# GroupNorm attention block on one core: score bursts of three units, one PSUM bank for all projection chains, x reloaded by blocks, VectorE in written order

## The chip, the cores and the metric

One NeuronCore of a Trainium2 chip runs the whole program. The metric is the device time of one execution in microseconds (us). TensorE (PE) does the matrix products, VectorE (DVE) the elementwise work, ScalarE (ACT) the exponentials, GpSimd (POOL) some small elementwise work and some DMA issues, SyncE (SP) most DMA issues. Each engine takes its instructions in order and waits on semaphores of the others.

## The reference

Four images of 512 channels and 48 x 48 = 2304 positions; eight heads of 64 channels.

```python
hn = _group_norm(x, gn_scale, gn_bias)                    # 32 groups of 16 channels
qkv = jnp.einsum('oc,bchw->bohw', qkv_w, hn) + qkv_b[None, :, None, None]
q, k, v = ...                                             # float16, (b, head, 64, 2304)
w = jnp.einsum('bhct,bhcs->bhts', q * scale, k * scale)
w = jax.nn.softmax(w, axis=-1)
a = jnp.einsum('bhts,bhcs->bhct', w, v).astype(jnp.float32)
out = jnp.einsum('oc,bchw->bohw', proj_w, a) + proj_b[None, :, None, None]
return x + out
```

## The kernel before, in words

`kernel` launches one program, in which `fast_path` does everything; `general_path` runs only if a softmax sum falls out of range, which does not happen here. The work is cut by image `b` (4), pair of heads `g` (16 in all, 4 an image) and block `j` of queries (`QBLOCKS`: four of 512 positions and one of 256).

**Attention.** A unit is one tile of 128 keys for both heads of a pair and 512 queries (for the block of 256 queries: two key tiles). `scores` makes the two matmuls of a unit (`ps`, a tile of two PSUM banks; the two heads use 64 rows of the array each), ACT's exp turns them into `p` (float16, 128x1024), and DVE adds `p` to `acc`. `values` multiplies `p` by `v` and accumulates in `av`, one PSUM bank for the whole block (here the two heads use 64 columns of the array each). A block of 512 queries has 18 units, the block of 256 has 9. Units come in bursts of two: PE gets the scores of burst n, then the values of burst n-1. After each six units `add_up` multiplies `acc` by ones into `sl` (a bank of its own) and `finish` copies the sums out, takes them through DRAM to spread them over partitions (`sums`, `row`, `ib`, all on SP's queue) and lets POOL scale the block (`att`).

**Work beside it.** Between bursts `fill` issues pieces from the list `beside[b]`, as many as keep a share of the list proportional to the place in the image: q and k chains of later pairs (`qk_items`: four steps over the channels into one bank `pw`, then a DVE eviction), v chains of the next image (`v_items`), projection chains of the image before (`proj_items`, eight float32r matmuls, a DVE add of bias and residual, a store). `pw` has two banks, `ps` two tiles (four banks), `av` and `sl` one bank each: eight in all.

**The turn between images.** `load_x` reloads x whole: four tiles of 2304 columns, each with one buffer, so its DMAs, issued from POOL, wait for the last q/k chain that reads the tile. `turn` puts the load and `norm_stats` after the chains of pair 3, `norm_apply` comes later in the list: `gmean` and `gvar` are matmuls in PE's order, and the v chains behind them need the normalised x.

**Order.** PE runs in the order in which the code issues (a manual schedule). All other engines' order is chosen by the scheduler.

Of the kernel before, what the change touches and what calls it, by code (L numbers as in the profile page):

```python
# [30 lines left out]
SCALE = float(np.float16(1.0 / math.sqrt(math.sqrt(D))))  # L31
LAG = 2
SUMMED = 6
# [10 lines left out]
SB = 384  # L44
# [422 lines left out]
def fast_path(  # L467
# [18 lines left out]
    apool = ctx.enter_context(tc.tile_pool(name="apool", bufs=7))  # L486
    ppool = ctx.enter_context(tc.tile_pool(name="ppool", bufs=6))
# [9 lines left out]
    def load_x(b, engines):  # L497
        chunks = []
        for c in range(NC):
            t = xpool.tile([P, T], F32, tag=f"x{c}", name=f"x_{b}_{c}")  # L500
            for h in range(2):
                cols = bass.ts(h, T // 2)
                engines[h].dma_start(t[:, cols], x[b, bass.ts(c, P), cols])
            chunks.append(t)
        return chunks

    hn = {0: load_x(0, (nc.sync, nc.scalar))}
# [28 lines left out]
    def split_wproj():  # L536
        for c in range(NC):
            w = work.tile([P, C], F32, tag="res", bufs=3, name=f"wproj_{c}")
            nc.sync.dma_start(w, proj_wT[bass.ts(c, P), :])
            nc.vector.tensor_copy(whi[:, c, :], w)  # L540
            nc.vector.tensor_tensor(
                wlo[:, c, :], w, whi[:, c, :].bitcast(F32), ALU.subtract
            )
# [22 lines left out]
    bqk = const.tile([P, 2 * NC], F32, name="bqk")  # L566
    nc.vector.tensor_scalar(bqk, bqkv[:, : 2 * NC], SCALE, None, ALU.mult)

    sums = const.tile([P, NG, 2 * NT], F32, name="sums")


    mvs = {}

    def norm_stats(b):
        mv = small.tile([P, NC, 2], F32, tag="mv", name=f"mv_{b}")
        for c in range(NC):
            st = small.tile([P, T // SB, 6], F32, tag="st", name=f"st_{b}_{c}")
            for j in range(T // SB):
                nc.vector.bn_stats(st[:, j, :], hn[b][c][:, bass.ts(j, SB)])  # L579
            nc.vector.bn_aggr(mv[:, c, :], st.rearrange("p j s -> p (j s)"))  # L580
        mvs[b] = mv

    def norm_apply(b):
        mv = mvs.pop(b)
        pm = ps_w.tile([P, NC], F32, tag="pw", name=f"gmean_{b}")
# [9 lines left out]
        pv = ps_w.tile([P, NC], F32, tag="pw", name=f"gvar_{b}")  # L595
# [11 lines left out]
        for o, n in QBLOCKS:  # L607
            for c in range(NC):
                t = hn[b][c][:, o : o + n]
                nc.vector.tensor_scalar(  # L610
                    t, t, ga[:, c : c + 1], gb[:, c : c + 1], ALU.mult, ALU.add
                )
# [4 lines left out]
    def qk_items(g):  # L617
        b, pr = divmod(g, NPAIR)
        items = []

        def new():
            qk[g] = [
                qkp.tile([P, T], F16, tag=n, name=f"{n}_{g}") for n in ("q", "k")
            ]

        def one(part, j, c, pw):
            o, n = QBLOCKS[j]
            if c == 0:
                pw[0] = ps_w.tile([P, QB], F32, tag="pw", name=f"pqk_{g}_{part}_{j}")
            w0 = part * C + pr * P  # L630
            for lo in (0, D):
                nc.tensor.matmul(  # L632
                    pw[0][lo : lo + D, :n],
                    wqkv[:, c, w0 + lo : w0 + lo + D],
                    hn[b][c][:, o : o + n],
                    start=(c == 0),
                    stop=(c == NC - 1),
                )
            if c == NC - 1:
# [3 lines left out]
                    pw[0][:, :n],  # L643
                    SCALE,
                    bqk[:, col : col + 1],
                    ALU.mult,
                    ALU.add,
                )

        items.append((0.0, new))  # L650
        for part in (1, 0):
            for j in range(NQ):
                pw = {}
                for c in range(NC):
                    items.append(
                        (
                            QBLOCKS[j][1] / 600.0,
                            lambda part=part, j=j, c=c, pw=pw: one(part, j, c, pw),
                        )
                    )  # L660
        return items
# [4 lines left out]
    def v_items(b):  # L666
        items = []

        def new():
            vv[b] = [  # L670
                vpool.tile([P, NT, C // 2], F16, tag=f"v{i}", bufs=1 + i, name=f"v{i}_{b}")
                for i in range(2)
            ]

        def one(i, c, pw):
            if c == 0:
                pw[0] = ps_w.tile([P, QB], F32, tag="pw", name=f"pv_{b}_{i}")
            for lo in (0, D):
                nc.tensor.matmul(  # L679
                    pw[0][lo : lo + D, :],  # L680
                    hn[b][c][:, i * P + lo : i * P + lo + D],
# [11 lines left out]
        items.append((0.0, new))  # L693
        for i in range(NT):
            pw = {}
            for c in range(NC):
# [109 lines left out]
    def add_up(g, j, m, per, last):  # L806
# [14 lines left out]
        if last:  # L821
            finish(g, j)
# [185 lines left out]
```

## Time and profile before

| | |
|---|---|
| median of 3 runs | 1920.93 us (1920.51 to 1924.32) |
| profiled execution | 1923.01 us, its span 1921.2 us |
| PE busy | 1725.2 us, 90% of the span |
| DVE, ACT, POOL busy | 1169.0, 1250.2, 180.2 us |
| mean granted TensorE clock | 0.978 of full speed |
| first scores start | 128.23 us |

The span runs from the first to the last instruction of the profiled execution. Busy time of PE is modelled from pipelined matmuls, so 90% is not 90% of its peak rate; the time from one group's start to the next group's start tells more than the busy time.

### The profile page before, as it was taken

How to read it: one execution, taken by the hardware profiler on the slowest of the kernel's cores; microseconds unless marked ns; L12 is line 12 of the kernel's file. 1: busy time of each engine (PE TensorE's matmuls, PEld its weight loads, DVE VectorE, ACT ScalarE, POOL GpSimd, SP SyncE). 2: the span in 40 equal slices, each digit the busy share in tenths (PEclk: the TensorE clock that was granted, in tenths of full speed). 3: DMA queues.
4: the chain of work that ended last, by engine and by line, in shares of the span. 5: the costliest groups of instructions: out<-in, count | busy, mean ns of one | idle time of the engine just before them, and what ended most of it. 6: DMA issues, size and time to landing. Idle time of an engine off the chain costs nothing.

```text
span 1921.2 us, 28172 instructions
## 1 busy us (share of the span) xinstructions
PE 1725.2 (90%) x10644; PEld 633.4 (33%) x10644; DVE 1169.0 (61%) x1936; ACT 1250.2 (65%) x1297; POOL 180.2 (9%) x204
## 2 busy tenths in 40 slices
PE   3999998599999998989999999789999998999875
PEld 1332323133333333433233332342323343333333
DVE  5236666666656657676665655767556665567654
ACT  0027777387777775667677767557777877778662
POOL 1000001100000001220000000221000011010111
PEclk9999999799999999999999999999999999999998
DMA  5000001100000003420000000540000021030223
GB/s 203 1 1 12 12 10 57 62 13 15 12 15 12 12 10 131 136 61 13 9 12 15 12 9 12 187 130 7 15 12 12 15 78 31 18 88 13 82 64 102
DMA packets 87730, 82.23 MB, mean 43 GB/s; under 512 B 50720, under 2 KB 56864, under 8 KB 87584
## 3 DMA queue, kind: packets, MB, share of 16 engines
q1 hardware_dynamic: 82848, 62.75, 11.8%
q0 software_dynamic: 3632, 14.18, 2.0%
q10 hardware_dynamic: 1104, 3.41, 0.5%
q8 instruction: 85, 1.39, 0.3%
q14 instruction: 61, 0.50, 0.1%
HBM read 60.83 MB, written 19.17 MB: 42 GB/s over the span
## 4 chain that ended last, share of the span: by engine, by line
PE 68%; ACT 10%; issue 8%; DVE 8%; DMA 5%; POOL 1%; SPq 0%; ACTq 0%; DVEq 0%; POOLq 0%
PE pqk L632 20%; PE ps L757 14%; PE av L792 12%; PE pv L679 10%; ACT p L765 10%; PE pr L720 7%; PE sl L814 3%; DVE acc L778 2%; DVE x L610 1%; DMA x<-x_dram 1%; DVE avx L801 1%; DMA wproj<-proj_wT_dram 1%; DMA sums<-slx 1%; DVE st L579 1%; DMA ib<-row 1%
## 5 line engine op out<-in xcount | busy, mean ns | idle before, releaser
L765 ACT ACTIVATE p<-ps 128x1024 f16<-128x1024 f32 x1296 | 1248.9, 1024 | 633.9 <-PE ps L757 628.0
L778 DVE TENSOR_TENSOR acc<-acc,p 128x1024 f16<-128x1024 f16 x848 | 611.4, 721 | 259.5 <-ACT p L765 242.8
L632 PE MATMUL pqk<-x,wqkv 128*64 128x512 f32 (+1 forms) x2560 | 564.1, 554 | 3.0 <-DVE x L610 2.9
L757 PE MATMUL ps<-q,k 64*128 64x512 f16 (+1 forms) x2880 | 434.7, 363 | 49.4 <-ACT p L765 37.6
L792 PE MATMUL av<-p,v 128*64 128x512 f16 (+1 forms) x2880 | 410.2, 368 | 59.3 <-DVE avx L801 58.8
L757 PEld LDWEIGHTS <-k 64*128 64x128 f16 x2880 | 116.7, 94 | 543.3 <-issue 535.2
L679 PE MATMUL pv<-wqkv,x 128*64 128x512 f32 x1152 | 276.4, 601 | 7.6 <-DVE x L610 7.6
L778 DVE TENSOR_TENSOR acc<-p,p 128x1024 f16<-128x1024 f16 x224 | 160.2, 715 | 179.0 <-ACT p L765 178.5
L844 POOL TENSOR_TENSOR att<-avx,ib 128x512 f16<-128x512 f32 (+1 forms) x80 | 106.5, 1331 | 1506.3 <-DMA ib<-row 1333.0
L632 PEld LDWEIGHTS pqk<-x,wqkv 128*64 128x64 f32 x2560 | 177.7, 138 | 185.1 <-issue 111.8
L792 PEld LDWEIGHTS <-v 128*64 128x64 f16 x2880 | 132.8, 109 | 249.5 <-issue 232.1
L720 PE MATMUL pr<-a,whi 128*128 128x512 f32 (+1 forms) x320 | 127.5, 406 | 11.2 <-POOL a L710 10.8
L720 PE MATMUL pr<-a,wlo 128*128 128x512 f32 (+1 forms) x320 | 119.1, 379 | 0.0
L679 PEld LDWEIGHTS pv<-wqkv,x 128*64 128x64 f32 x1152 | 81.1, 139 | 113.2 <-issue 82.4
L814 PE MATMUL sl<-acc,ones 128*64 128x512 f16 (+1 forms) x512 | 92.1, 377 | 0.1
L727 DVE SCALAR_TENSOR_TENSOR x<-pr,bproj,x 128x512 f32<-128x512 f32 (+1 forms) x80 | 55.6, 695 | 59.6 <-PE pr L720 45.7
L689 DVE TENSOR_TENSOR v<-pv,bv 128x256 f16<-128x256 f32 x144 | 55.9, 417 | 54.9 <-PE pv L679 54.5
L828 DVE COPY slx<-sl 128x512 f32<-128x512 f32 (+1 forms) x80 | 50.9, 637 | 51.6 <-PE sl L814 50.2
L720 PEld LDWEIGHTS pr<-a,whi 128*128 128x128 f32 x320 | 61.8, 193 | 46.6 <-issue 16.7
L641 DVE TENSOR_SCALAR q<-pqk,bqk 128x512 f16<-128x512 f32 (+1 forms) x80 | 55.4, 693 | 27.6 <-PE pqk L632 26.8
L641 DVE TENSOR_SCALAR k<-pqk,bqk 128x512 f16<-128x512 f32 (+1 forms) x80 | 55.2, 690 | 19.3 <-PE pqk L632 18.2
L801 DVE COPY avx<-av 128x512 f32<-128x512 f32 (+1 forms) x80 | 50.8, 635 | 26.0 <-PE av L792 25.7
(46 smaller groups left out, 288.9 us busy)
## 6 DMA issues: line engine op xcount, KB each, us to landing
x<-x_dram SPq DMA_DIRECT2D x64, 256.0 KB, 2.9
ib<-row SPq DMA_DIRECT2D x128, 128.0 KB, 3.0
out_dram<-x SPq DMA_DIRECT2D x64, 256.0 KB, 2.4
x<-x_dram POOLq DMA_DIRECT2D x24, 576.0 KB, 7.1
x<-x_dram ACTq DMA_DIRECT2D x4, 576.0 KB, 11.0
x<-x_dram SPq DMA_DIRECT2D x4, 576.0 KB, 10.7
wqkv<-qkv_wT_dram SPq DMA_DIRECT2D x2, 1024.0 KB, 15.9
sums<-slx SPq DMA_DIRECT2D x128, 2.0 KB, 2.0
```

What stands on the lines that cost most here:

```text
L632: nc.tensor.matmul(pw[0][lo : lo + D, :n], wqkv[:, c, w0 + lo : w0 + lo + D], hn[b][c][:, o : o + n], start=(c == 0), stop=(c == NC - 1),)
L641: nc.vector.tensor_scalar(qk[g][part][:, o : o + n], pw[0][:, :n], SCALE, bqk[:, col : col + 1], ALU.mult, ALU.add,)
L679: nc.tensor.matmul(pw[0][lo : lo + D, :], hn[b][c][:, i * P + lo : i * P + lo + D], wqkv[:, c, 2 * C :], start=(c == 0), stop=(c == NC - 1),)
L689: nc.vector.tensor_tensor(vv[b][half][:, i, :], pw[0][:, cols], bv[:, cols], ALU.add)
L720: nc.tensor.matmul(ps[:, :n], w[:, c, bass.ts(m, P)], at[0][:, c, :n], start=(c == 0 and i == 0), stop=(c == NC - 1 and i == 1),)
L757: nc.tensor.matmul(ps[:, h, a * n : (a + 1) * n], k[rows, bass.ts(i, P)], q[rows, o : o + n], start=True, stop=True,)
L765: nc.scalar.activation(pt, ps, AF.Exp)
L778: nc.vector.tensor_tensor(acc[key], before, pt, ALU.add)
L792: nc.tensor.matmul(av[0][lo : lo + D, :n], vv[b][pr // 2][:, i, pr % 2 * P + lo : pr % 2 * P + lo + D], pt[:, h, a * n : (a + 1) * n], sta ...
L801: nc.vector.tensor_copy(avx[g, j][:, :n], av[0][:, :n])
L814: nc.tensor.matmul(sl[0][lo : lo + D, :n], ones16, t[:, h, a * n : (a + 1) * n], start=(m < SUMMED and a == 0), stop=(last and a == per - 1),)
L844: nc.gpsimd.tensor_tensor(atts[g][:, o : o + n], avx.pop((g, j))[:, :n], ib[:, :n], ALU.mult)
```

## The change

The diff touches almost all of `fast_path`; its core:

```diff
+BURST = 3
-SUMMED = 6
-    apool = ctx.enter_context(tc.tile_pool(name="apool", bufs=7))
-    ppool = ctx.enter_context(tc.tile_pool(name="ppool", bufs=6))
+    apool = ctx.enter_context(tc.tile_pool(name="apool", bufs=6))
+    ppool = ctx.enter_context(tc.tile_pool(name="ppool", bufs=3))
...
-    ps_s = ctx.enter_context(tc.tile_pool(name="ps_s", bufs=2, space=PSUM))
+    ps_s = ctx.enter_context(tc.tile_pool(name="ps_s", bufs=3, space=PSUM))
     ps_av = ctx.enter_context(tc.tile_pool(name="ps_av", bufs=1, space=PSUM))
-    ps_l = ctx.enter_context(tc.tile_pool(name="ps_l", bufs=1, space=PSUM))
-    ps_w = ctx.enter_context(tc.tile_pool(name="ps_w", bufs=2, space=PSUM))
...
+    ps_w = ctx.enter_context(tc.tile_pool(name="ps_w", bufs=1, space=PSUM))
...
+    def load_x(b, j, engines):
...
+        o, n = QBLOCKS[j]
         for c in range(NC):
...
+            t = xpool.tile([P, n], F32, tag=f"x{c}_{j}", name=f"x_{b}_{c}_{j}")
+            engines[c % len(engines)].dma_start(t, x[b, bass.ts(c, P), o : o + n])
+            hn[b, c, j] = t
...
+    alone = [True]
+
+    def chain_bank(name):
+        if alone[0]:
+            return ps_s.tile([P, 2, QB], F32, tag="ps", name=name)[:, 0, :]
+        return ps_w.tile([P, QB], F32, tag="pw", name=name)
...
     def scores(u):
...
+        pt = ppool.tile([P, BURST, 2, QB], F16, tag="p", name=f"p_{g}_{j}_{k}")
+        for r in range(BURST):
+            ps = ps_s.tile([P, 2, QB], F32, tag="ps", name=f"ps_{g}_{j}_{k}_{r}")
...
+            nc.scalar.activation(pt[:, r], ps, AF.Exp)
...
+    def add(u):
...
+        if k == 1:
+            acc[g, j] = work.tile(
+                [P, BURST, 2, QB], F16, tag="acc", bufs=1, name=f"acc_{g}_{j}"
+            )
+        nc.vector.tensor_tensor(acc[g, j], before, pt, ALU.add)
+
+    def add_up(g, j):
+        o, n = QBLOCKS[j]
+        per = QB // n
+        sl = chain_bank(f"sl_{g}_{j}")
...
         for j in range(NQ):
+            for part in (1, 0):
+                put(b, qk_chain(g + 3, part, j), per_pair - 1, g + 3)
+            put(b, [piece(0.0, lambda b=b, j=j: load_x(b + 1, j, (nc.gpsimd,)))])
+            if j > 1:
+                put(b, [piece(0.0, lambda b=b, j=j: stats(b + 1, j - 2))])
...
+    def fill(n, close):
...
+            if after > place or (first and ended):
+                break
+            if done[b] > share and not (close and open_chain[0]):
+                break
...
+        if 0 < n <= len(stream):
+            values(stream[n - 1])
+            add(stream[n - 1])
+        if ended(n - 3):
+            divide(*stream[n - 3][:2])
+        if ended(n - 2):
+            add_up(*stream[n - 2][:2])
+        else:
+            fill(n, ended(n - 1))
...
-    with tc.manual_schedule(engines={mybir.EngineType.PE}):
+    with tc.manual_schedule(engines={mybir.EngineType.PE, mybir.EngineType.DVE}):
```

What it does, in words. Bursts have three units in three `ps` tiles (six banks); `acc` and `p` are 3072 columns wide, so one DVE add takes a burst. `sl` is made once a block, from the 3 x 2 slices of `acc`, and uses the one bank `pw`, which all q, k, v and projection chains share. A `fill` ends at most one chain, and a burst that has an `add_up` has no `fill`. Where the attention is not running (`alone`: the start and the end), chains use the `ps` tiles. x lies in 20 tiles by block, each reloaded as soon as the q and k chains of pair 3 on its block are issued; `stats` follows two blocks later, then `group_mean`, `group_var`, and `norm` block by block among the v chains. Projection chains fetch their residual two chains ahead. The split of the projection weights (`split_wproj`) is spread over the first pair. The range test of the sums is four small POOL instructions a block. DVE, too, runs in the order of the code.

PE, pair 1 of image 0, the boundary between query blocks 1 and 2 (`av_1_1` and `av_1_2`; numbers after the last underscore are buffers; each pair of load and matmul stands twice, once a head). Before:

```order
L757 MATMUL ps_1_2_2_1885<-q_1_632,k_1_633 128x512
L632 MATMUL pqk_3_1_2_1891<-x_0_0_99,wqkv_115 64x512 x2
...
L792 MATMUL av_1_1_1694<-p_1_1_17_1863,v0_0_319 64x512
L792 LDWEIGHTS v0_0_319
L792 MATMUL av_1_2_1898<-p_1_2_0_1869,v0_0_319 64x512
...
L757 MATMUL ps_1_2_3_1901<-q_1_632,k_1_633 128x512
```

The same place in the changed kernel:

```order
L820 MATMUL av_1_1_1646<-p_1_1_5_1768,v0_0_336 64x512
L655 MATMUL pqk_3_0_1_1788<-x_0_3_1_110,wqkv_140 64x512 x2
L796 LDWEIGHTS k_1_552
L796 MATMUL ps_1_2_1_0_1829<-q_1_551,k_1_552 128x512
...
L796 MATMUL ps_1_2_1_1_1833<-q_1_551,k_1_552 128x512
...
L796 MATMUL ps_1_2_1_2_1837<-q_1_551,k_1_552 128x512
...
L820 MATMUL av_1_2_1841<-p_1_2_0_1795,v0_0_336 64x512
```

The first values of the new block stood right behind the last of the old one; now the rest of a chain and the scores of three units stand between them. In PE's order of the kernel before, 40 of the 80 blocks begin inside a burst in this way.

DVE, the turn from image 1 to image 2. Before (`st`: statistics, `acc`: additions, `avx`: copy of `av`):

```order
L778 TENSOR_TENSOR acc_5_3_0_6009<-acc_5_3_0_6009,p_5_3_2_6014 128x1024
L579 BN_STATS st_2_0_6033<-x_2_0_6020 128x6 x3
L727 SCALAR_TENSOR_TENSOR x_0_0_0_6071<-pr_0_0_0_6070,bproj_114,x_0_0_0_6071 128x512
L579 BN_STATS st_2_0_6033<-x_2_0_6020 128x6 x3
L579 BN_STATS st_2_1_6041<-x_2_1_6023 128x6
L580 BN_AGGR mv_2_6032<-st_2_0_6033 128x2
L579 BN_STATS st_2_1_6041<-x_2_1_6023 128x6 x2
L801 COPY avx_5_2_6085<-av_5_2_5821 128x512
L579 BN_STATS st_2_1_6041<-x_2_1_6023 128x6 x3
```

The same turn in the changed kernel (`q_7`, `k_7`: the last chains that read image 1's x; the fourth number of x is its block):

```order
L664 TENSOR_SCALAR q_7_5551<-pqk_7_0_4_5962,bqkv_138 128x256
L589 BN_STATS st_2_5786<-x_2_0_2_5778 128x6
...
L853 TENSOR_TENSOR acc_5_3_5874<-acc_5_3_5874,p_5_3_4_5942 128x3072
L743 SCALAR_TENSOR_TENSOR r_0_3_0_5465<-pr_0_3_0_6011,bproj_139,r_0_3_0_5465 128x512
L829 COPY avx_5_3_6049<-av_5_3_5836 128x512
L853 TENSOR_TENSOR acc_5_3_5874<-acc_5_3_5874,p_5_3_5_5991 128x3072
L743 SCALAR_TENSOR_TENSOR r_0_3_1_5498<-pr_0_3_1_6052,bproj_139,r_0_3_1_5498 128x512
L589 BN_STATS st_2_5786<-x_2_0_3_5900 128x6
...
L872 COPY slx_5_3_6108<-sl_5_3_6101 128x512
L853 TENSOR_TENSOR acc_5_4_6144<-p_5_4_0_6024,p_5_4_1_6069 128x3072
L888 RECIPROCAL inv_5_3_6152<-sums_5_3_6110 128x8
```

The statistics of a whole image stood almost in a row, a burst's work between them; now four of one block stand between the adds and evictions of several bursts, and the reciprocal, which waits for a DMA, has a fixed place behind an add.

## Rows read from the trace of the kernel before

**Rows 1.** The page: busy time, share and count of each engine.
```profile
PE 1725.2 (90%) x10644; PEld 633.4 (33%) x10644; DVE 1169.0 (61%) x1936; ACT 1250.2 (65%) x1297; POOL 180.2 (9%) x204
```
**Rows 2.** Timeline of PE, 700 to 722 us: start us, us, group [idle before <-releaser].
```profile
702.85 0.60 PE L757 MATMUL ps<-q,k 64*128 64x512 f16 x4
703.38 0.62 PE L792 MATMUL av<-p,v 128*64 128x512 f16 x4
703.84 1.88 PE L632 MATMUL pqk<-x,wqkv 128*64 128x512 f32 x8
705.65 0.61 PE L757 MATMUL ps<-q,k 64*128 64x512 f16 x4
...
719.90 0.39 PE L792 MATMUL av<-p,v 128*64 128x512 f16 x2
721.35 0.41 PE L792 MATMUL av<-p,v 128*64 128x512 f16 x2 [1.06 <-DVE avx L801]
```
**Rows 3.** Waits of PE, 128 to 1890 us: total us, times, longest us.
```profile
PE av L792 <- DVE avx L801: 58.8, 41, 7.3
PE ps L757 <- ACT p L765: 37.6, 82, 0.9
PE gmean L586 <- DVE mv L580: 20.1, 1, 20.1
```
**Rows 4.** Windows: length, busy by engine (count), granted clock, DMA share, GB/s.
```profile
330.00:360.00 30.00, 6.42 (x42) 2.80 (x40) 20.00 (x50) 3.46 (x4) 5.44 (x8) 0.56 0.46 167
...
1200.00:1300.00 100.00, 81.36 (x478) 41.71 (x478) 72.46 (x132) 53.07 (x57) 23.62 (x31) 0.93 0.48 152
```
**Rows 5.** Timeline of all engines, first turn, 328 to 352 us.
```profile
328.68 1.28 POOL L503 DMA_DIRECT2D x<-x_dram  x2 [14.33 <-PE pqk L632]
...
342.95 1.63 POOL L503 DMA_DIRECT2D x<-x_dram  x3
347.01 1.48 DVE L579 BATCH_NORM_STATS2 st<-x 128x6 f32<-128x384 f32 x3 [4.96 <-DMA x<-x_dram]
...
351.96 0.59 PE L586 MATMUL gmean<-mv,gmat 128*128 128x4 f32 x2 [20.10 <-DVE mv L580]
```
**Rows 6.** Timeline of all engines, the start and the first scores.
```profile
21.81 0.56 PE L586 MATMUL gmean<-mv,gmat 128*128 128x4 f32 x2 [21.81 <-DVE mv L580]
26.22 0.43 DVE L540 CAST whi<-wproj 128x512 fp32r<-128x512 f32 x1 [4.55 <-DMA wproj<-proj_wT_dram]
...
29.89 0.59 PE L596 MATMUL gvar<-var,gmat 128*128 128x4 f32 x2 [7.51 <-DVE var L594]
...
33.42 33.07 PE L632 MATMUL pqk<-x,wqkv 128*64 128x512 f32 x160 [2.95 <-DVE x L610]
...
128.23 0.61 PE L757 MATMUL ps<-q,k 64*128 64x512 f16 x4
```
**Rows 7.** Timeline of all engines, last image, 1871 to 1890 us.
```profile
1871.03 0.39 PE L720 MATMUL pr<-a,whi 128*128 128x512 f32 x1
...
1872.89 0.40 PE L720 MATMUL pr<-a,whi 128*128 128x512 f32 x1
...
1876.72 0.60 PE L757 MATMUL ps<-q,k 64*128 64x512 f16 x4
...
1877.21 7.44 ACT L765 ACTIVATE p<-ps 128x1024 f16<-128x1024 f32 x8 [8.98 <-PE ps L757]
...
1886.50 1.15 SPq L832 DMA_DIRECT2D sums<-slx  x2
...
1889.21 0.20 DVE L834 RECIPROCAL inv<-sums 128x8 f32<-128x8 f32 x1 [0.40 <-DMA sums<-slx]
...
1889.76 1.07 ACT L765 ACTIVATE p<-ps 128x1024 f16<-128x1024 f32 x1
```
**Rows 8.** Groups by form: count, busy us, mean ns, idle before us, releasers.
```profile
L778 DVE TENSOR_TENSOR acc<-acc,p 128x1024 f16<-128x1024 f16 x848 | 611.4, 721 | 259.5 <-ACT p L765 242.8 <-DVE acc L778 0.5 <-DVE inv L834 0.2
L778 DVE TENSOR_TENSOR acc<-p,p 128x1024 f16<-128x1024 f16 x224 | 160.2, 715 | 179.0 <-ACT p L765 178.5
...
L641 DVE TENSOR_SCALAR q<-pqk,bqk 128x512 f16<-128x512 f32 x64 | 47.8, 746 | 22.7 <-PE pqk L632 21.8
...
L641 DVE TENSOR_SCALAR q<-pqk,bqk 128x256 f16<-128x256 f32 x16 | 7.7, 478 | 5.0 <-PE pqk L632 5.0
```
**Rows 9.** The chain that ended last: start us, us, what.
```profile
66.50 61.80 PE pv L679 x288
```

More of the change, by code (lines that the diff above doesn't have):

```diff
@@ L824, in finish @@
-    def finish(g, j):
+                    sl[lo : lo + D, :n],
+                    ones16,
+                    t[:, r, h, a * n : (a + 1) * n],
+                    start=((r, a) == steps[0]),
+                    stop=((r, a) == steps[-1]),
+                )
+        sx = work.tile([P, QB], F32, tag="rows", name=f"slx_{g}_{j}")
+        nc.vector.tensor_copy(sx[:, :n], sl[:, :n])
+        sums[g, j] = small.tile([P, 2, QB // P], F32, tag="sums", name=f"sums_{g}_{j}")
+        for h in range(2):
+            nc.sync.dma_start(sums[g, j][:, h, : n // P], sx[h * D : h * D + 1, :n])
@@ new lines, in fast_path, with issue @@
+    done = dict.fromkeys(range(B), 0.0)
+    open_chain = [False]
+    def issue(b):
+        us, run, first, last, _, _ = beside[b].pop(0)
+        run()
+        done[b] += us
+        open_chain[0] = (open_chain[0] or first) and not last
+    def fill(n, close):
+        b, place = min(n // per_batch, B - 1), n
+        place = n - b * per_batch
+        share = total[b] * (place + 1) / (per_batch - 2)
+        ended = False
+        while beside[b]:
+            _, _, first, last, after, _ = beside[b][0]
+            if after > place or (first and ended):
+                break
+            if done[b] > share and not (close and open_chain[0]):
+                break
@@ L931, in fast_path @@
-    for u in waiting:
-        values(u)
-    while late:
-        late.pop(0)()
+    ended = lambda n: 0 <= n < len(stream) and stream[n][3]
+    for n in range(len(stream) + 4):
+        if n < len(stream):
+            wanted(stream[n][0])
+            scores(stream[n])
+        else:
+            alone[0] = True
+        if 0 < n <= len(stream):
[5 more added lines that the diff above has]
+            add_up(*stream[n - 2][:2])
+        else:
+            fill(n, ended(n - 1))
@@ L948, in fast_path @@
-    pf = ps_w.tile([1, 1], F32, tag="pw", name="count")
-    for i in range(2):
-        nc.tensor.matmul(
-            pf, good[:, i : i + 1], ones, start=(i == 0), stop=(i == 1)
-        )
-    nc.vector.tensor_scalar(flag, pf, float(B * HEADS * T) - 0.5, None, ALU.is_lt)
+    good = small.tile([P, 1], F32, tag="good", bufs=1, name="good")
+    nc.vector.tensor_reduce(good, fine.rearrange("p h i -> p (h i)"), AX.X, ALU.add)
+    pf = chain_bank("count")[:1, :1]
+    nc.tensor.matmul(pf, good, ones, start=True, stop=True)
@@ L956, in group_norm_attention @@
+    nc.vector.tensor_scalar(flag, pf, float(2 * QB) - 0.5, None, ALU.is_lt)
 @with_exitstack
```

498 lines of the change are left out of this document (253 added, 245 removed).

## The prediction

> **What bounds the kernel now.** I read the page first [rows 1]: PE is busy for 1725 of 1921 us, ACT for 1250 and DVE for 1169. So PE bounds it; but what its busy time is made of, the timeline shows better. I price PE's work by the distance between starts. In the first image's v chains nothing waits: 288 records, which are 18 chains of four channel steps, take 61.80 us [rows 9], 0.858 us for a step (four records) and 3.43 for a chain. A step streams 512 columns four times, a float16 pair of matmuls (both heads) once: 0.215 us a pair. A projection matmul takes 0.2325 us (1871.03 to 1872.89 is eight of them), a chain 1.86 [rows 7].
>
> In a calm stretch a burst of two units starts at 702.85 and the next at 705.65 [rows 2], 2.80 us. Its work is two score pairs, two value pairs (0.86) and two steps (1.72), 2.58. The other **0.22 us** lie where the array changes its shape: the scores use it as 64*128, all else as 128*64 or whole, and from ps to av it takes 0.53 us for 0.43 of columns. There are 648 bursts.
>
> The attention runs from 128.23 us [rows 6] to the end of the last exp, 1890.83 [rows 7]; less the last burst's own 2.4 us it is 1760 us for 647 bursts. I count PE's work in it in PE's order: 16 x 81 units, 15 pairs of q/k chains, three images of v chains, 70 projection chains, the `sl` matmuls. It comes, by the sum below, to 1375 us in both kernels. Bursts cost 647 x 0.22 = 142. So **243 us are waits** or work at a lower clock. The waits of PE name the large ones [rows 3]: 58.8 us for the copy of `av`, 37.6 for ACT, and 20.1 in one piece at the first turn between images. There [rows 4] PE works 6.4 of 30 us and the granted clock is 0.56 of full, so for most of the time the lower of its levels, 1.2 of 2.4 GHz, after PE had stopped; the third turn (1200 to 1300) still loses 19 us and has a clock of 0.93. The chain of that first stop [rows 5]: the x loads wait for the last q chain, POOL issues the last three only at 342.95 after a scaling that waited for a DMA, DVE waits 4.96 us for them, and `gmean` at 351.96 ends PE's 20 us, since it stands next in PE's order.
>
> **The change part by part.**
>
> *Bursts of three.* 431 bursts and a last one instead of 647: 216 x 0.22 = **-47 us**. If the 0.22 us belonged to matmuls and not to bursts, nothing: that bound is kept for the range.
>
> *The start of a block's values.* The 40 blocks that begin inside a burst wait for the copy of `av`, 1.06 us at 721.35 [rows 2], 58.8 us in all. Now a burst's scores (0.65 us at least) and mostly a chain stand between; the copy is next on DVE when the values end and takes what a row of like shape takes, under 0.75 us [rows 8]. I take **-55**.
>
> *x by blocks.* A block's tile is free after its own chains, so four of the five blocks of x are there while the last chains run, and only 256 columns come late. Between the last q chain and the first v chain the new PE order has five bursts without a chain in the first turn, and in each of the others thirteen, eight of them with a projection chain. Bursts keep PE going where it stood, at ACT's pace. For the late statistics and `norm` I keep 25 us over three turns.
>
> *Short bursts.* This is the price. ACT takes 0.917 us a unit (8 in 7.44, the last one 1.02 long) [rows 7], 2.75 for three. An exp starts 0.49 us after its scores [rows 7]. After a long burst ACT is idle when the scores come, so a short one lasts until the third exp frees its tile: 0.49 + 3 x 0.92, less the two score pairs that go ahead of the third, some 2.97 us; after another short one 2.75. In the new PE order 154 bursts of 431 have less work: 79 with `add_up` and no fill (six pairs and `sl`: 1.29 + 0.65 + 0.22 = 2.16), 40 with a quarter of a chain (2.37), 21 bare ones (1.51), 12 with a short projection chain. Filled up to 2.75 that is 95 us, to 2.97 it is 128. Long bursts go mostly ahead of short ones, but the tail is a row of short ones: I take **115**. It takes the place of the 37.6 us for ACT and of the like waits inside burst groups.
>
> *DVE's adds.* 352 adds of 3072 columns replace 1072 of 1024, which took 772 us [rows 8]. No row has this size. Above, three single ones are 3 x 0.72 = 2.16 us; below, a second and third save the fixed part, which two evictions of 512 and 256 columns put at 0.746 - 2 x 0.268 = 0.21 us, so 1.74. An add is nearer to three that follow without a gap; I take 1.8, 634 us in all. DVE has some 1030 us of work in 1780 and waits for ACT most, so the saving is worth nothing by itself; what matters is that an eviction can stand behind 1.8 us of add.
>
> *One bank.* All 353 chains and `sl` groups of the attention use one bank, so each waits for the eviction of the one before, 0.746 us [rows 8]. A fill ends one chain at most, so a burst's scores and the values before them, 1.29 + 0.22 us, always stand between. The add in front of the eviction starts when the third exp of its burst ends, about when the next scores do, so 1.8 us later it is over, while the values and a chain (0.65 + 1.86 or more) still run. I cost it at nothing: the cover is 1.5 us against 0.75. Bound: all of it in the open, 353 x 0.746 = 263 us.
> The Trainium skill, page "Perfetto Trace Analysis", section "Optimizing Tensor Performance", speaks against this edit: independent matmul groups should rotate through PSUM banks, so that the eviction of one lies beside the next one's matmuls. By the rule the sum would gain those 263 us; by the rows other matmuls lie there. It is a rival below.
>
> *DVE in written order; divisions.* A reciprocal waits for the DMA of the sums: issued at 1886.50, it is used at 1889.21, 2.71 us [rows 7]. It now stands behind an add, which covers 1.8 of them; some 0.9 us are left, 80 times, behind which a chain's eviction may wait. As that chain ends later (values and chain again), I cost it at nothing, 72 us as the bound.
>
> *Start.* `gmean` is done at 22.4, but `gvar` waits until 29.89, because DVE first does the weight split, whose DMA lands at 26.2; the first chain starts at 33.42 [rows 6]. Without the split, four small operations (about 0.2 us each) lie between, so some 6 us go; the rest stays. First scores near **121.5** instead of 128.2. Loads by blocks may give 2 us more, weights that land later take as much.
>
> *Nothing else:* the same number of exps; residuals fetched earlier, POOL's range test and its 60 loads for 24 lie on engines that wait (POOL 9% busy [rows 1]); the tail's division takes the same DMAs.
>
> **The sum.** Work: 431 x 6 pairs x 0.215 = 556; 120 q/k chains of 3.43 and 30 of half = 463; 54 v chains = 185; 58 projection chains of 1.86 and 12 of about half = 119; 79 `sl` of 0.645 = 51; together 1375 (rounded up by 1). Bursts 431 x 0.22 = 95. Short bursts 115. Left over 45: 25 for the turns, 20 of what is lost now at a lower clock and between engines (of the 243 us, 136 are named by the waits, the rest is mostly short bursts and clock). That makes 1630. With 121.5 ahead, 3.3 for the last burst and the same 30.4 after the last exp: a span of 1785, against 1921.2. Outside the span lie 1923.01 - 1921.2 = 1.8 us: **1787 us**. The profiled execution stood 2 us over the median of 1920.93, which I leave in the rounding: 1786.
>
> **The rivals.**
>
> *A: as summed*, 1745 to 1825. For it speak the idle stretches, which need only be filled.
>
> *B: half of it.* Either the 0.22 us belong to the matmuls (1786 + 47 = 1833), or the reciprocals and statistics hold up DVE's fixed order and the chains behind them: 1786 + 72 = 1858. For it: behind a reciprocal that waits, nothing can now be brought forward, and the adds are more than twice as long. Against: ps to av takes 0.1 us more than its columns.
> The Trainium skill, "Perfetto Trace Analysis", section "Optimizing Scalar/DVE Operations", advises to break up instructions where DVE is not saturated but makes others wait, the opposite of the wide add; no row here has the wide add yet.
>
> *C: better.* Short bursts hide behind long ones and the turns cost nothing: 1786 - 20 - 25 = 1741 or less.
>
> *D: no change*: the turns stay as they are (24 us idle in the first and 19 in the third [rows 4], the second taken between, 65 in all) and B's 72 come on top: 1923.
>
> *E: slower: the one bank in the open.* If each of the 353 uses of `pw` waits for its eviction, 1786 + 263 = 2049. It decides from 135 / 353 = 0.38 us each on, which would take DVE some 1.2 us behind at every chain. This is what the skill's rule on banks would do here. For it: all chains in one bank, and DVE's order fixed. Against: the 1.5 us of other matmuls, and DVE idle for over a third of the time.
>
> **How the numbers follow.** A 0.62, B 0.24, C 0.05, D 0.03, E 0.06. The time is A's. The range of 1745 to 1880 leaves out C, a fifth of B, D and E, 0.19. 0.2%, some 4 us, is about what a measurement of this kernel tells from no change: the runs shown spread by 3.8. Faster by more: A, B, C, 0.91; within: 0.03; slower: 0.06.
>
> **What would show it.** Right: first scores near 121; no wait of `av` for `avx` over some us in all; at the three turns PE works at ACT's pace with a clock near 1.0, no stop of 20 us; waits of `ps` for ACT grown to about 100 us; adds near 1.8 us; a burst with a whole q chain at about 4.94 us. Wrong: waits of `pqk`, `pv`, `pr` or `sl` for a DVE eviction beyond 30 us in all (E), or DVE's wait for sums, statistics or residuals in front of them (B); a burst's extra still at 0.33 us for three units (B).

## The result, and the profile after

The changed kernel takes 1801.46 us (median; 1798.37 to 1801.77), the one before 1922.62 on the same chip: a ratio of 0.9365, 95% interval 0.9347 to 0.9383. Forecast were 1786 us and a range of 1745 to 1880. The profiled execution took 1798.37, its span is 1796.6 us.

The page, where [rows 1] stood before: busy time of each engine, and the granted clock in 40 slices in tenths.

```profile
PE 1652.7 (92%) x10706; PEld 649.1 (36%) x10706; DVE 1030.8 (57%) x1194; ACT 1220.1 (68%) x1297; POOL 334.7 (19%) x561
...
PEclk9999999999999999999999999999999999999998
```

PE's waits in the attention, where [rows 3] stood: total us, times, longest.

```profile
PE ps L796 <- ACT p L803: 63.1, 140, 0.5
PE gmean L596 <- DVE mv L594: 10.4, 3, 7.5
PE pr L735 <- DVE r L743: 10.3, 10, 3.2
...
PE pr L735 <- POOL a L727: 3.4, 4, 0.9
PE pqk L655 <- DVE k L664: 2.0, 3, 0.9
...
PE av L820 <- DVE avx L829: 0.6, 1, 0.6
```

The wait of `av` for its copy is gone (58.8 to 0.6), and `gmean`'s 20-us stop is now one of 7.5. What is left is named by ACT: short bursts. On PE's timeline, a long burst, a short one (it has the `sl` matmuls and no chain) and the next long one, each from its first scores to those of the next:

```profile
1323.57 0.82 PE L796 MATMUL ps<-q,k 64*128 64x512 f16 x6
...
1328.53 0.82 PE L796 MATMUL ps<-q,k 64*128 64x512 f16 x6
...
1330.70 0.64 PE L796 MATMUL ps<-q,k 64*128 64x512 f16 x4
1331.87 0.39 PE L796 MATMUL ps<-q,k 64*128 64x512 f16 x2 [0.52 <-ACT p L803]
...
1336.39 0.82 PE L796 MATMUL ps<-q,k 64*128 64x512 f16 x6
```

The first takes 4.96 us, the short one 2.17, and the third 5.69 for the same work as the first: its third scores wait for ACT. The burst is 0.73 us longer, of which the row of waits shows 0.52; the row counts from a modelled end of the matmul before, the distance between starts doesn't.

The first turn in windows of 10 us (length, busy time of PE, PEld, DVE, ACT, POOL with counts, granted clock, DMA share, GB/s), where [rows 4] stood:

```profile
300.00:310.00 10.00, 4.73 (x40) 1.78 (x34) 9.61 (x17) 5.71 (x6) 3.67 (x7) 0.96 0.34 79
310.00:320.00 10.00, 6.81 (x40) 3.07 (x42) 6.98 (x20) 5.19 (x6) 1.04 (x1) 0.53 0.01 2
320.00:330.00 10.00, 7.24 (x78) 3.86 (x75) 7.19 (x10) 8.80 (x10) 0.84 (x4) 1.00 0.03 1
```

PE was idle for half of ten microseconds while DVE was 96% busy, and behind that the clock was granted at 0.53 of full, near the lower of its two levels (1.2 of 2.4 GHz); that is the old stop, smaller. What DVE did, and what PE waited for:

```profile
304.60 6.14 DVE L589 BATCH_NORM_STATS2 st<-x 128x6 f32<-128x512 f32 x12
...
313.19 0.56 PE L596 MATMUL gmean<-mv,gmat 128*128 128x4 f32 x2 [7.52 <-DVE mv L594]
```

The start and the first scores, timeline, where [rows 6] stood (start us, us, instruction, [idle before <-releaser]):

```profile
19.57 0.56 PE L596 MATMUL gmean<-mv,gmat 128*128 128x4 f32 x2 [19.57 <-DVE mv L594]
...
20.98 0.59 PE L610 MATMUL gvar<-var,gmat 128*128 128x4 f32 x2 [0.84 <-DVE var L604]
...
25.96 1.97 PE L655 MATMUL pqk<-x,wqkv 128*64 128x512 f32 x4 [4.40 <-DVE x L628]
...
120.48 0.61 PE L796 MATMUL ps<-q,k 64*128 64x512 f16 x4
```

The end, timeline, where [rows 7] stood; the last exp ends at 1759.50:

```profile
1761.26 1.75 DVE L853 TENSOR_TENSOR acc<-acc,p 128x3072 f16<-128x3072 f16 x1
...
1763.07 0.84 PE L864 MATMUL sl<-acc,ones 128*64 128x256 f16 x12 [0.19 <-DVE acc L853]
...
1765.18 1.19 SPq L876 DMA_DIRECT2D sums<-slx  x2
...
1777.26 0.72 POOL L898 TENSOR_TENSOR att_last<-avx,ib 128x256 f16<-128x256 f32 x1 [1.30 <-DMA ib<-row]
```

The last sums leave 5.7 us after the last exp. Before, that took 1.7:

```profile
1892.51 1.99 SPq L832 DMA_DIRECT2D sums<-slx  x2
```

**Where the time came from.** The same units of work can be timed in both kernels: from the start of the scores of one unit (on PE's timeline) to that of a later one. Eight stretches, counted in the bursts of the changed kernel (three units each):

| bursts | before, us | after, us | saved | what lies there |
|---|---|---|---|---|
| 0 to 40 | 152.0 | 148.4 | 3.6 | first q/k chains |
| 40 to 76 | 159.8 | 149.6 | 10.2 | first turn |
| 76 to 130 | 208.3 | 200.8 | 7.5 | |
| 130 to 190 | 267.3 | 248.3 | 19.0 | second turn, projections |
| 190 to 238 | 190.4 | 187.5 | 2.9 | |
| 238 to 298 | 269.6 | 245.7 | 23.9 | third turn, projections |
| 298 to 346 | 179.2 | 173.9 | 5.3 | |
| 346 to 431 | 332.3 | 281.0 | 51.3 | last image, projections |

The four stretches with neither a turn nor projections save 19 us of 730; the other 104 us were saved in the turns and in the last image.

The largest piece is one that I hadn't priced by itself. At the end of the last image the old list gave out the four projection chains of a block in one burst (8.5 us of PE work in the burst, ACT idle for up to 11.8 us) and left the other bursts bare, at ACT's pace. The new `fill` ends one chain a burst: the part from burst 404 on takes 87.3 us instead of 112.8 (and 111.6 again in experiment 4, where `fill` may end more than one).

### The profile page after: what moved, and what is told of

Read it like the earlier page. It is cut to its first block, busy times and chain, and to the rows that moved or that the text cites. A ratio compares the mean times of both kernels' runs of the same rounds, so it can differ in the third digit from the quotient of the medians.

```text
span 1796.6 us, 26704 instructions
## 1 busy us (share of the span) xinstructions
PE 1652.7 (92%) x10706; PEld 649.1 (36%) x10706; DVE 1030.8 (57%) x1194; ACT 1220.1 (68%) x1297; POOL 334.7 (19%) x561
## 5 line engine op out<-in xcount | busy, mean ns | idle before, releaser
L803 ACT ACTIVATE p<-ps 128x1024 f16<-128x1024 f32 x1296 | 1218.8, 1038 | 523.6 <-PE ps L796 523.4
L655 PE MATMUL pqk<-x,wqkv 128*64 128x512 f32 (+1 forms) x2560 | 530.4, 551 | 6.4 <-DVE x L628 4.4
L853 DVE TENSOR_TENSOR acc<-acc,p 128x3072 f16<-128x3072 f16 x272 | 482.3, 1773 | 31.0 <-ACT p L803 29.5
L796 PE MATMUL ps<-q,k 64*128 64x512 f16 (+1 forms) x2880 | 388.2, 360 | 64.0 <-ACT p L803 63.1
L820 PE MATMUL av<-p,v 128*64 128x512 f16 (+1 forms) x2880 | 363.7, 366 | 0.6 <-DVE avx L829 0.6
L885 POOL TENSOR_SCALAR in<-sums 128x8 f32<-128x8 f32 (+1 forms) x160 | 55.1, 345 | 964.3 <-DMA sums<-slx 957.9
L820 PEld LDWEIGHTS <-v 128*64 128x64 f16 x2880 | 125.6, 109 | 188.9 <-issue 149.6
L853 DVE TENSOR_TENSOR acc<-p,p 128x3072 f16<-128x3072 f16 x80 | 145.1, 1814 | 24.8 <-ACT p L803 24.7
L735 PE MATMUL pr<-a,whi 128*128 128x512 f32 (+1 forms) x320 | 126.1, 401 | 19.2 <-DVE r L743 10.3
L664 DVE TENSOR_SCALAR k<-pqk,bqkv 128x512 f16<-128x512 f32 (+1 forms) x80 | 55.7, 696 | 109.4 <-PE pqk L655 109.4
L664 DVE TENSOR_SCALAR q<-pqk,bqkv 128x512 f16<-128x512 f32 (+1 forms) x80 | 55.6, 696 | 105.1 <-PE pqk L655 105.1
L743 DVE SCALAR_TENSOR_TENSOR r<-pr,bproj,r 128x512 f32<-128x512 f32 (+1 forms) x80 | 55.4, 693 | 47.6 <-PE pr L735 37.8
```

What stands on the lines that cost most here:

```text
L655: nc.tensor.matmul(pw[0][lo : lo + D, :n], wqkv[:, c, w0 + lo : w0 + lo + D], hn[b, c, j], start=(c == 0), stop=(c == NC - 1),)
L664: nc.vector.tensor_scalar(qk[g][part][:, o : o + n], pw[0][:, :n], bqkv[:, col : col + 1], SCALE, ALU.add, ALU.mult,)
L735: nc.tensor.matmul(ps[:, :n], w[:, c, bass.ts(m, P)], at32[b, j][:, c, :n], start=(c == 0 and i == 0), stop=(c == NC - 1 and i == 1),)
L743: nc.vector.scalar_tensor_tensor(xt, ps[:, :n], bproj[:, m : m + 1], xt, ALU.add, ALU.add)
L796: nc.tensor.matmul(ps[:, h, a * n : (a + 1) * n], kt[rows, bass.ts(i, P)], qt[rows, o : o + n], start=True, stop=True,)
L803: nc.scalar.activation(pt[:, r], ps, AF.Exp)
```

## The experiments

All times are medians beside runs of the kernel before on the same chip; ratios are to that. A repeated stretch is alike to 0.1 us in several of these kernels (148.4, 200.8 and 173.9 us come again and again), so small effects are read there and not from the total. Where a burst's length is given, it is the distance from the start of its first scores to that of the next burst, and "class" means the PE work that stands in the burst in PE's order.

**1. Is the 0.22 us a price of the burst?** (e1_switch)

```diff
-            scores(stream[n])
+            scores(stream[n], (0, 1))
...
-            values(stream[n - 1])
+            values(stream[n - 1], (0,))
+            scores(stream[n], (2,))
+            values(stream[n - 1], (1, 2))
```

> The same work with one more change of shape and back in each burst: the scores of units 1 and 2, the values of one unit, the scores of unit 3, the values of the other two. If the 0.22 us of a burst belong to its two changes of the array's shape (scores as 64*128, the rest as 128*64), 432 bursts have two more of them: up to 432 x 0.22 = 95 us more than the 1801 of the changed kernel, less what the short bursts (154) hide, since they wait for ACT anyway: 61 us from the 277 long ones. So 1860 to 1896. Rival: the 0.22 us belong to the matmuls or to a burst's bookkeeping; then 1801 within 6 us.

1824.81 us, ratio 0.9495 (0.9465 to 0.9524): 23 us more, far below the bounds of the first theory and outside those of the rival. The bursts themselves are clear, though. The medians of the classes in which nothing waits go from 2.18 to 2.40 (with `sl`), 2.38 to 2.61 (a quarter of a chain), 3.25 to 3.47 (half a q/k or v chain), 4.10 to 4.32 and 4.96 to 5.18 (a whole chain): 0.22 us for one more change of shape and back, each time. One such burst, the one that takes 4.96 us above, here 5.18:

```profile
1345.04 0.60 PE L798 MATMUL ps<-q,k 64*128 64x512 f16 x4
...
1350.22 0.60 PE L798 MATMUL ps<-q,k 64*128 64x512 f16 x4
```

The matmuls are the same and only their order is another, so the price belongs to the change of shape, not to the matmuls. What the expectation lacked is a gain: the third scores now come after the values of a unit, when ACT has freed their tile, and PE's wait for ACT falls from 63.1 us to

```profile
PE ps L798 <- ACT p L805: 9.1, 31, 0.5
```

**2. The same only behind short bursts** (c1_split_short): `split = beside_us < 1.0`, the work beside the pairs of the burst before.

> The scores of unit 3 come after the values of unit 1, as in the run e1_switch, but only in the 154 bursts that follow a burst with under 1 us of work beside its pairs. In e1_switch the bursts in which nothing waits grew by just 0.22 us (2.18 to 2.40, 4.96 to 5.18), which is 95 us over 432, and the whole by 24, so some 70 us came back from the wait of ps for ACT (63 to 9 us). If the two are independent, 154 x 0.22 = 34 us are paid and up to 70 come back: 1801 - 36 = 1765, 1758 to 1775, and the wait of ps for ACT is under 15 us. Rival: the wait only moves to the next burst's first scores or to the values (ACT has 2.75 us to do in any case): 1801 to 1835.

1786.18 us, ratio 0.9296 (0.9273 to 0.9320): 15 us less than the changed kernel, in the direction of the theory and less than half of its size; time and wait both miss what was expected. The wait of `ps` for ACT is 21.6 us in 93 waits, so 41 came back by the rows and 154 x 0.22 = 34 were paid; that gives 8. Between starts a wait costs some 0.2 us more than its row shows, and there are 47 fewer, about 9 us by this estimate, which brings it to 17. The full 70 us came only with the split in every burst: the third burst shown above (5.69 us) takes 5.48 here and 5.25 in experiment 1. Short bursts are a real cost, but this cure pays 34 us to win back about 50.

**3. A chain in the burst with `sl`** (e7_slfill): `add_up` ahead of `values`, and `fill` in every burst.

> In the burst with add_up the sl matmuls go ahead of the values, their copy ahead of the burst's add, and a chain may follow, so 79 bursts of 2.17 us of PE work become longer and others shorter. The work that PE has over 2.75 us floors falls from 95 to 77 us by the rows' prices. If the short bursts are what the ACT waits (63 us of ps for p) and the long bursts after sl (5.75 for 4.94) come from, the time falls by 18 to 35 us: 1766 to 1783. Rival: the chain then waits for the copy of sl in the one bank, 0.7 us at up to 63 places, and sl for the add before it: 1801 to 1845.

1830.78 us, ratio 0.9523 (0.9494 to 0.9552): the rival, 29 us slower, although PE's list of work is more even. One place, on the timeline:

```profile
409.14 1.75 DVE L853 TENSOR_TENSOR acc<-acc,p 128x3072 f16<-128x3072 f16 x1
...
410.80 0.75 DVE L706 TENSOR_TENSOR v<-pv,bv 128x256 f16<-128x256 f32 x2
...
411.61 0.84 PE L864 MATMUL sl<-acc,ones 128*64 128x512 f16 x6 [1.05 <-DVE v L706]
...
412.76 0.68 DVE L872 COPY slx<-sl 128x512 f32<-128x512 f32 x1
...
413.49 3.65 PE L696 MATMUL pv<-wqkv,x 128*64 128x512 f32 x16 [0.40 <-DVE slx L872]
```

`sl` waits for the eviction of the chain before, which stands behind the wide add, and the next chain waits for the copy of `sl`: the one bank in the open, twice in a burst. Up to 1766 us such waits of `sl` come to 30 us in all, against 4 in the changed kernel.

**4. Two ends in a burst** (e8_fill2): the break at `first and ended` goes from `fill`.

```diff
-            if after > place or (first and ended):
+            if after > place:
```

> A fill may end one chain and begin the next in the same burst, so at 117 places two uses of the one bank follow without scores and values between; the work is the same, and by the rows' prices the short bursts cost the same 94 us. If the one bank costs nothing only because a burst's pairs lie between two uses, each such place now shows the eviction, 0.75 us of it and some 0.3 of semaphores, and 1.8 us more where an add is ahead of it: 117 x 0.9 to 117 x 1.9 less what ACT's waits hide, so 1850 to 1960. Rival: evictions are quick enough, or PE makes the time up in the next bursts: 1801 within 15 us.

1971.02 us, ratio 1.0241 (1.0213 to 1.0269): slower than the kernel before, and 11 us above the range of the first theory. PE's waits:

```profile
PE pqk L655 <- DVE k L664: 42.5, 32, 3.5
PE pqk L655 <- DVE q L664: 31.6, 30, 2.3
PE pv L696 <- DVE v L706: 30.6, 25, 2.4
PE pr L735 <- DVE r L743: 21.1, 21, 3.1
```

With three smaller rows of the kind (3.4, 2.2, 1.7) 133 us, 1.1 us for each of the 117 places; the granted clock is 0.973 instead of 0.991, and the lumps of projections in the last image are back (bursts 416, 422 and 428 take 14.9 us each). The prediction's rival E is thus a real mechanism, and the rule of one end a burst is what holds it off.

**5. DVE's order left to the scheduler** (e4_dve_free): `engines={PE}` only.

> VectorE's order is chosen by the scheduler, as before the change; TensorE's stays written. If the wait of av for avx (58.8 us before, 0.6 now) went because scores and a chain now stand between, it stays gone and the time is 1801 within 10 us. Rival: it went because the written order puts the copy first on VectorE; then av's wait comes back by 20 to 59 us, 1821 to 1860. Third: the written order costs (inv waits for sums 93 us at the head of VectorE's row, pr for r 10 us); then 1785 to 1793.

1879.17 us, ratio 0.9776 (0.9754 to 0.9798): 78 us of the 121 are gone, more than any of the three cases foresaw. PE's waits:

```profile
PE pqk L655 <- DVE k L664: 32.2, 17, 6.6
...
PE pr L735 <- DVE r L743: 15.5, 19, 2.5
PE pqk L655 <- DVE q L664: 9.0, 12, 1.0
...
PE av L820 <- DVE avx L829: 0.6, 1, 0.6
```

The wait of `av` stays gone, so PE's order removed it, as predicted. What comes back is the one bank: `pqk` waits 41 us for the evictions of q and k, against 2.0, and with smaller rows of the kind (`pv` for `v` 6.1, `pr` for `r` 15.5, three more of 4.8 together) all chains wait 68 us for evictions, against 12. One of these waits, timeline:

```profile
274.05 4.48 DVE L853 TENSOR_TENSOR acc<-acc,p 128x3072 f16<-128x3072 f16 x2
...
278.45 0.74 DVE L664 TENSOR_SCALAR k<-pqk,bqkv 128x512 f16<-128x512 f32 x1
...
279.24 4.49 PE L655 MATMUL pqk<-x,wqkv 128*64 128x512 f32 x12 [4.63 <-DVE k L664]
```

Ahead of the adds, DVE had waited 3.5 us for the x of the next image's statistics, which the scheduler had put there; two adds and the eviction came late behind them. The head is lost too: the first scores start at 128.72, because the weight split stands again between `gmean` and `gvar` (30.75 instead of 20.98).

**6. That order alone, on the kernel before** (e12_before_dve): `engines={PE, DVE}` there.

> The kernel before with one part of the change alone: VectorE in written order. In the changed kernel leaving that order out cost 78 us. If the order is worth as much by itself (evictions and av's copy no longer behind statistics and adds): 1922 - 30 to 1922 - 80, 1842 to 1892. If it needs the x tiles by block and the spread statistics: the 20 statistics of the next image, all issued at one place, now hold VectorE's row until the whole x is there, some 20 to 30 us three times, and PE and ACT stop with it: 1922 to 2000. Third: the wait of av (58.8 us) was a matter of the order alone: then it falls under 10 us here.

2019.27 us, ratio 1.0500 (1.0481 to 1.0519). DVE's waits, and PE's:

```profile
DVE inv L834 <- DMA sums<-slx: 225.6, 78, 6.6
```

```profile
PE av L792 <- DVE avx L801: 97.4, 40, 14.9
...
PE sl L814 <- DVE acc L778: 24.9, 35, 1.9
```

The old code issues the reciprocal right behind the transfer of the sums. In written order it holds DVE's row 2.9 us, 78 times (29.3 us in all before), and the adds, the copies of `av` and the evictions with it; every one of the eight stretches gets longer, by 4 to 30 us, those without a turn too. At two turns all 24 statistics of the next image stand in one row (12 us of work) ahead of `av`'s copy, and PE waits 13.9 and 14.9 us. So the order isn't a gain by itself. In the changed kernel `divide` comes a burst after `add_up` and the statistics are spread; that these two are what makes the order pay there is likely by the rows above, but no run takes either of them away from it.

**7. Divisions a burst later** (e2_div4): `ended(n - 4)`.

> The reciprocal of a block's sums (divide) comes one burst later in the written order of VectorE, so the sums have 3 to 5 us more to arrive. If what the reciprocals hold up is only what PE's own waits show (10.3 us of pr for r, 10 waits, and the lower clock behind the long ones), the time falls by 8 to 15 us: 1786 to 1793, and inv's wait for sums falls from 93 us to under 20. Rival (B of the prediction, 72 us): the reciprocals hold up the fixed order throughout, and the projection bursts (58 of them 44 us over their work) with it: 1730 to 1765. Third: the waits are covered altogether and the bursts after a block's sl only wait for ACT: 1801 within 4 us.

1794.49 us, ratio 0.9329 (0.9301 to 0.9358). The intervals overlap; the stretches tell more: from the first scores to the last exp 1628.3 us instead of 1639.0, 9.0 and 6.2 less in the second and third turn, alike within 0.7 elsewhere but for the last image, which takes 4.1 more, since its own projections now wait for the attention (`pr` for POOL's `a` 15.4 us instead of 3.4). `pr` waits 0.4 us for `r`, not 10.3, and DVE's wait for the sums falls from 93.1 us to 0.2. That is the mechanism and the size of the first theory (8 to 15 us) in the stream, 10.7; the total, 7 us less, lies 1.5 us outside its range, as the end takes 7 us more, 44.1 from the last exp. One place in the changed kernel, second turn, shows what went:

```profile
672.46 0.20 DVE L888 RECIPROCAL inv<-sums 128x8 f32<-128x8 f32 x1 [5.31 <-DMA sums<-slx]
...
672.59 0.75 DVE L743 SCALAR_TENSOR_TENSOR r<-pr,bproj,r 128x512 f32<-128x512 f32 x1
...
673.39 0.50 PE L735 MATMUL pr<-a,whi 128*128 128x512 f32 x1 [3.25 <-DVE r L743]
```

The eviction `r` stands behind a reciprocal that waits for its sums, and the next projection chain waits for `r`. Even so the bursts with a projection chain have a median of 3.60 for 3.38 of priced work. A chain that uses the array whole adds 0.22 to its burst, as experiment 1's change of shape did; that it is the same cause is likely, not shown.

**8. Statistics spread over more bursts** (e5_turns).

```diff
-            for i, r in zip(reversed(chains[1:8:2]), reversed(rest)):
+            for i, r in zip(reversed(chains[0:7:2]), reversed(rest)):
...
-            for r in rest:
-                put(b, r)
-        put(b, [piece(0.0, lambda b=b: norm(b + 1, 0))])
+            for i, r in enumerate(rest):
+                put(b, r, 49 + 2 * i)
+        put(b, [piece(0.0, lambda b=b: norm(b + 1, 0))], 0 if b else 56)
```

> The statistics of the next image are spread: in the first turn the last two blocks' statistics, gmean, gvar and the first scaling come two bursts apart (bursts 49, 51, 53, 55, 56 of the image), in the other turns one projection chain earlier each. If the three stops (7.5 us for mv at burst 49, two bursts of 9.9 instead of 4.9 us, and the lower clock after each) come from PE reaching these small matmuls before DVE and POOL are through, they go: 15 to 22 us less than 1801, so 1779 to 1786, and no gmean wait over 1 us. Rival: the late x transfers set the time, and the stop moves with the statistics: 1801 within 4 us.

1796.79 us, ratio 0.9339 (0.9309 to 0.9368): the theory fell. The first turn takes 151.6 us (149.6), the others 246.4 (248.3) and 245.3 (245.7). The stop is still there, in another place:

```profile
319.44 0.20 DVE L888 RECIPROCAL inv<-sums 128x8 f32<-128x8 f32 x1 [1.05 <-DMA sums<-slx]
...
319.56 0.69 DVE L594 BATCH_NORM_AGGREGATE mv<-st 128x2 f32<-128x30 f32 x4
...
320.39 0.56 PE L596 MATMUL gmean<-mv,gmat 128*128 128x4 f32 x2 [3.14 <-DVE mv L594]
320.89 1.46 PE L796 MATMUL ps<-q,k 64*128 64x512 f16 x6
```

`mv` stands behind a reciprocal that waits for its sums, `gmean` waits 3.14 us for it, and the scores after it run at the lower clock (1.46 us for 0.82). In this turn, which has only bare bursts beside the statistics, moving the small matmuls gained nothing.

**9. x loaded late** (e9_x_late): the loads and early statistics after the loop over the blocks.

> x still lies in tiles by block, but all loads of the next image are issued after the last q and k chains of pair 3 instead of each behind its own block's chains. If the early loads are what shortened the first turn, its statistics wait for 4.7 MB that start some 20 us later: 20 to 40 us more, 1821 to 1845, nearly all in the first turn, since eight projection chains cover the others. Rival: the place of the statistics and of gmean in the written order did it: 1801 within 6 us.

1816.80 us, ratio 0.9448 (0.9426 to 0.9469): 15 us more, somewhat under the first theory, and not where it said: 3.6, 6.2 and 7.2 us in the three turns, the least in the first. So 17 us of the 53 saved in those three stretches hang on the early loads and the early statistics, which this edit moves together.

**10. The wide add cut in three** (e6_add3).

> The wide add of 3072 columns is three of 1024 again, in the written order. VectorE then has 352 x (3 x 0.72 - 1.78) = 134 us more work, and a chain's eviction stands behind 2.16 us instead of 1.78; the first two can start before the third exp. If the width costs or saves nothing on the path: 1801 within 5 us. If evictions are near the path (10 us of pr for r, 3 to 8 of sl and pqk): up to 352 x 0.1 = 35 us more. Rival, the advice to break up wide instructions: the last add is 1.06 us shorter than the wide one, evictions come earlier and the waits of pr for r and the like, some 15 us, go: 1786 to 1795.

1804.39 us, ratio 0.9376 (0.9358 to 0.9393): no difference that can be told. PE's waits are those of the changed kernel within some 3 us each. The width of the add is neutral.

**11. Four edits together** (c2_combo).

```diff
+        for late in (3, 4):
+            if ended(n - late) and (stream[n - late][0] == NG - 1) == (late == 3):
+                divide(*stream[n - late][:2])
...
+    def tail_queue():
+        return nc.scalar if alone[0] else nc.sync
```

> Four edits together on the changed kernel, each read in a stretch of its own: the split scores behind short bursts (15 us by its run); divisions one burst later except in the last pair, whose late division cost 4 us in its projections and 7 in the tail of the run e2_div4 (15 us in the second and third turn stay); statistics one projection chain earlier in these turns (2 to 4 us); the sums, row and ib transfers of the last block from ACT's queue, which is idle behind the last exp, instead of SP's behind stores and residuals (3 us of a tail of 37). If they add up: 1801 - 15 - 15 - 3 - 3 = 1765, 1758 to 1772. Rival: the waits of projection bursts are the same ones that the split takes away, so that they don't add: 1775 to 1786.

1771.47 us, ratio 0.9205 (0.9187 to 0.9222): the best version, 30 us under the changed kernel; just inside the expected range, above its centre. Against the split alone the second and third turns give 5.2 and 6.4 us. The queue gave nothing: the end takes 40.7 us, and it is between 35.5 and 40.4 in the nine kernels that have the changed kernel's divisions and queues there. The last `row` is issued at 1739.50 and `ib` follows at 1744.24, on an idle queue; so these two waits are for the transfers to land, not for SP's queue.

## Why the prediction was right, and where it was off

**The sum against the spans.** Predicted 1785 for the span, measured 1796.6: the start 1.0 us early (120.48), 431 bursts in 1635.2 instead of 1630, the last burst 3.9 instead of 3.3, the end 37.1 instead of 30.4. The signs: first scores, the wait of `av`, the adds and a burst with a whole q chain (4.96 us) came as said. The first turn still stopped PE, and the clock fell there. The wait of `ps` for ACT is 63 us by its row, not about 100; with the 0.2 us that a wait costs above its row, 140 times, it would be some 90.

**Bursts, 47 us:** right as a price; 0.22 us for each change of shape and back (experiment 1). No run has the changed kernel with bursts of two, so what three units a burst are worth, less the short bursts that come with them, isn't shown.

**The start of a block's values, 55 us:** right, 58.2 by the waits, and by PE's order alone (experiment 5).

**x by blocks and turns:** "I keep 25 us over three turns". The three stretches with a turn gained 53 us and still lie some 48 us over their floor (each burst at its priced PE work or at 2.75, whichever is more: 137.4, 229.0, 229.0 against 149.6, 248.3, 245.7), projection bursts included. What the early loads and statistics give is 17 of the 53 (experiment 9). That "bursts keep PE going at ACT's pace" failed in the first turn: DVE had twelve statistics in a row there, and the clock fell.

**Short bursts, 115 us, and the 45 left over:** right together, less so apart. Bursts at their work or at 2.75 us cost 94 over the work, my lower bound; what lies above that is 72 us, 48 of it in the stretches with turns and 14 in the last image. In the other four stretches 66 short bursts cost 45 us over their work, 0.68 each, where 115 over 154 is 0.75: short bursts were priced nearly right, and the 45 left over were some 60. The upper figure of 2.97 us doesn't follow from its own terms (0.49 + 3 x 0.92 - 0.43 is 2.82); the place shown above has 2.17 + 0.73 = 2.90.

**Adds, 1.8 us:** 1.77 and 1.81, in groups by form:

```profile
L853 DVE TENSOR_TENSOR acc<-acc,p 128x3072 f16<-128x3072 f16 x272 | 482.3, 1773 | 31.0 <-ACT p L803 29.5
L853 DVE TENSOR_TENSOR acc<-p,p 128x3072 f16<-128x3072 f16 x80 | 145.1, 1814 | 24.8 <-ACT p L803 24.7
```

The Trainium skill's advice to break such an instruction up ("Perfetto Trace Analysis", section "Optimizing Scalar/DVE Operations") would have changed nothing here (experiment 10).

**One bank at nothing:** right in the sum, since the chains' and `sl`'s waits for a chain's eviction come to some 15 us of a bound of 263. The reason was incomplete. The cover needs two things that I named and didn't price: one end a burst (without it 170 us, 133 of them named by waits for evictions, experiment 4) and an eviction that comes next behind the add (without the written order 70 us between first scores and last exp, of which some 55 are longer waits for evictions, experiment 5). The Trainium skill's rule to rotate banks ("Perfetto Trace Analysis", section "Optimizing Tensor Performance") is right about the danger, and experiment 4 has it in the open; the changed kernel keeps the evictions beside other matmuls in another way.

**DVE's order and the divisions at nothing:** the divisions cost about 11 us in the stream (experiment 7), of a bound of 72. B's sign did come, though: DVE stands before reciprocals for their sums,

```profile
DVE inv L888 <- DMA sums<-slx: 88.9, 76, 5.3
```

but most of that is covered. The order itself I took for a risk; without it 78 of the 121 us are gone, 8 of them at the start (experiment 5).

**The tail, "the same 30.4 after the last exp":** the largest of the four differences above. I costed the transfers and left out that the last `sl` now waits for a wide add behind the copy of `av` (1761.26 to 1763.07) and that a projection's eviction and residual lie between: the sums leave 4 us later, the last block is scaled 17.8 us after the last exp instead of 13.1.

**Not in my sum:** the 25 us at the end of the last image. They were in the 243 us of waits that I took away as a whole, so the total held without the reason. That is in part luck: by the prices of the sum experiment 4's order costs the same within 2 us (1561 against 1563, short bursts at 2.75), although the lumps are back there and it takes 1811.

Of the rivals, B's first half (0.22 belongs to the matmuls) is refuted by experiment 1 and its second by experiment 7; E didn't happen, but half a line less in `fill` makes it (experiment 4).

## What to carry to other kernels

One PSUM bank for many chains was nearly free here, as long as other matmuls stood between two uses and the eviction had a sure place on its engine; the orders of the two engines belong together (VectorE's alone made the old kernel slower, and without it most of the gain was gone). In a written order an instruction that waits for a DMA round trip holds everything behind it, so it belongs a burst or two after its transfer. Even out the work beside a paced engine, one chain a burst; lumps and bare bursts each cost, and a time for the same units in both kernels shows where better than totals of waits do.

## What the runs showed that was not expected

A change of the array's shape and back costs 0.22 us in every class of burst in which nothing waits, to 0.01 us. The third scores of a burst, put behind one unit of values, take away 54 of 63 us of waiting for ACT at that price.

A POOL instruction next to a DVE add can be slow, and the add with it. In the kernel of experiment 5 two adds run beside POOL's work from 274.05 on: the first takes its usual 1.74 us, the second 2.63. POOL's scaling of `att` beside them takes 2.79, where 1.26 is seen in the changed kernel (1766.48), and the cast behind it 2.02, where 0.61 is seen (1767.81). No experiment here took this apart.
